# Attention block on one NeuronCore: queries and keys laid out token by token, and score and context matmuls spread between projection halves

## The chip, the core and the metric

The kernel runs on one core of one Trainium2 chip. The metric is the device time of one execution in microseconds (us). Three runs of the kernel before gave 2223.61, 2233.66 and 2239.39 us; the median is 2233.66 us. One further execution was taken by the hardware profiler; its own time was 2238.77 us and its span, from the first to the last instruction, 2236.9 us.

## What is computed

One pre-layernorm transformer block on 2048 tokens of width 1024, in float32. The attention is unusual: it is taken within each token, between its 32 heads, not between tokens. Each token thus has a 32 x 32 score matrix of its own.

```python
def attention(x):                                   # x: (1, 2048, 1024), already normalised
    q = (x @ wq.T + bq).reshape(B, S, 32, 32)       # heads h, head width d
    k = (x @ wk.T + bk).reshape(B, S, 32, 32)
    v = (x @ wv.T + bv).reshape(B, S, 32, 32)
    scores = einsum('bshd,bstd->bsht', q, k) / sqrt(32)
    return einsum('bsht,bstd->bshd', softmax(scores), v).reshape(B, S, 1024)

x = x + attention(layernorm(x))
h = layernorm(x)
x = x + (silu(h @ dq(w1).T) * (h @ dq(w2).T)) @ dq(w3).T   # hidden width 2752
```

Here dq rounds a weight to the 16 values of the NF4 code, per block of 64 elements with the block's largest magnitude as scale. The kernel does this rounding itself, on the chip.

## The kernel before

The program has two stages. The **attention stage** takes the first 617 us of the profiled execution, the **FFN stage** the rest. A third kind of work, the rounding of the FFN weights (the "background"), runs beside both.

**Tiles.** Tokens come in 16 tiles of 128. For tile i, `load_x` brings x into one of three `xt` buffers. `prepare(i)` normalises it into `xn` with three passes on ACT (ScalarE) and small steps on POOL (GpSimd). `split(i)` transposes `xn` on PE (TensorE) in eight blocks through two PSUM banks; ACT copies the result rounded to the shorter float32r format into `xh` (line 620) and DVE (VectorE) writes what the rounding lost into `xl` (line 621).

**Projections.** `Q(i, n)`, `K(i, n)` and `V(i, n)` each make one half (512 columns) of the queries, keys or values: 16 matmuls (line 648), for eight chunks of the input width and for both parts xh and xl, into one PSUM bank. Four banks go round for these halves, for the transposes of `split` and `keep`, and for the transposes of background weights (`ptw`). After the 16 matmuls the half is taken out: DVE transposes it in 32 x 32 blocks from PSUM to SBUF (line 665 for queries and keys, line 678 for values) and, after the second half, adds the bias. Queries and keys lie in `qd` and `kd` as 128 partitions x 32 x 32: in a group of 32 partitions the partition is the head width, the first free index is the head and the second the token. Values in `vd` lie with the token first, and each token has a 33rd column of ones, so that the context matmul also makes the softmax's sum.

**Scores and contexts.** `S(i, part)` issues 64 matmuls of 32 x 32 (line 696), one per token and group of 32 partitions; part 0 and part 1 are the halves of a tile. It reads `q[r, :, s]` and `k[r, :, s]`, that is, 32 elements 128 bytes apart in each partition. After part 1, DVE takes the maxima (line 733), subtracts them (line 735), ACT takes the exponential (line 741) and DVE transposes the result into `prT` (line 743). `G(i, part)` issues 64 matmuls (line 700) that weigh the values; after part 1, DVE divides by the sums (lines 758, 760), transposes into `cx` (line 768), adds the residual (line 771); SP, the queue of the loads and stores, writes x1 out and loads the next x tile; ACT and POOL normalise `cx`. Scores and contexts of all tiles use one PSUM tile `at` of four banks, one after the other. In the trace each of the 64 float32 matmuls has two records, so that a part appears as x128.

**Keep.** `keep(i)` transposes the normalised `cx` on PE (line 511), copies it out on ACT (line 512) and, for every second tile, forms four differences on DVE (line 527); all go to DRAM as operands of the FFN, which multiplies 2 x 2 blocks with seven products in place of eight.

**Background.** `advance(n)` issues n x 10/17 steps of the weight rounding: a pass of ACT (line 299) and one of DVE (lines 303, 305) for each of eight bands of code values, block maxima (line 271), reciprocals and scalings (lines 255, 259). A call of `advance` follows each projection half and each part of scores or contexts. `flush(1)` issues one piece of the finishing of a rounded weight: four transposes on PE (line 219) with a copy on ACT (line 220), or the differences on DVE (lines 226 to 235) and the store.

**What sets the order.** On PE the instructions run in the order in which the program writes them. On the other engines a planner places them, from the program's dependences; each engine then works through its own list in order. The order written for a tile i from 3 to 14 is

`prepare(i+1)  Q(i,0)  Q(i,1)  keep(i-2)  K(i,0)  G(i-1,0)  K(i,1)  G(i-1,1)  V(i,0)  S(i,0)  V(i,1)  split(i+1)  S(i,1)`

with `flush(1)` before `keep`, before `G(i-1,1)` and before `split`. After the loop, the first products of the FFN (`plain_block`, each `next` one group of four matmuls of line 391) alternate with `keep(14)`, `G(15, .)` and `keep(15)`. There, after `G(15,1)`, `held["behind"]` makes background steps start only behind the last normalisation. The first full FFN unit follows; its first sum is copied by ACT to `g` (line 1416).

A second, slower path of the same function serves inputs that the short format can't hold; it isn't run with these inputs. The profile numbers lines as in the listing.

## Time and profile before

| stretch, us from the start of the span | length | PE busy | DVE busy | ACT busy | granted PE clock |
|---|---|---|---|---|---|
| attention stage, 0 to 617 | 617.0 | 573.7 | 450.9 | 352.6 | 0.96 |
| of it twelve tiles, 145.48 to 566.50 | 421.0 | 398.9 | 327.5 | 238.4 | 0.97 |
| of it the end, 566.50 to 600 | 33.5 | 30.0 | 10.9 | 7.0 | 0.90 |
| into the FFN, 600 to 640 | 40.0 | 31.8 | 25.1 | 30.2 | 0.87 |
| FFN stage, 617 to 2237 | 1620.0 | 1593.4 | 927.2 | 934.6 | 0.99 |
| profiled execution, span | 2236.9 | 2167.1 | 1378.0 | 1287.2 | 0.98 |
| profiled execution, its own time | 2238.8 | | | | |

Busy time is the time in which an engine has at least one instruction under way. The granted clock is the mean share of full speed at which TensorE was allowed to run; in the trace it is either 1 or one half. A tile of the twelve is counted from its first score matmul to that of the next tile. In lines of groups, the name before the arrow is what is written, the names behind it what is read; then come sizes and count, busy time and mean nanoseconds of one, and the idle time of the engine just before with what ended it.

### The profile page before, as it was taken

The page shows a single profiled execution, that of the slowest core. Times are in us where ns is not written, and L with a number is a line of the kernel's source. Part 1 is how long each engine was busy: PE and PEld are TensorE (multiplying, and loading weights), DVE is VectorE, ACT ScalarE, POOL GpSimd, SP SyncE. Part 2 cuts the span into 40 slices and gives each one's busy share as a digit, 9 for nine tenths or more (in the row PEclk, how much of TensorE's full clock was granted, in tenths as well). Part 3 has the DMA queues.
Part 4 walks back from the last instruction along what each step waited for, and adds up shares of the span by engine and source line. Part 5 has one row for each costly group of instructions (what it writes and reads, how often), then busy time and mean ns, then how long its engine had stood idle before and what let it go on. Part 6 is the DMA issues. An engine that isn't in the chain of part 4 may idle for free.

```text
span 2236.9 us, 35174 instructions
## 1 busy us (share of the span) xinstructions
PE 2167.1 (97%) x14193; PEld 1173.4 (52%) x14193; DVE 1378.0 (62%) x1600; ACT 1287.2 (58%) x2529; POOL 302.2 (14%) x425
## 2 busy tenths in 40 slices
PE   7999999989989999999999999999999999999998
PEld 6777787778534444444444444444444444444432
DVE  6778777786377565576565665756666656653022
ACT  7566665662285756758657666676586575511200
POOL 2010010100001203104012021040130210401300
PEclk9899999999999999999999999999999999999999
DMA  8132323234558837579349596394883776974972
GB/s 292 40 101 93 117 65 115 95 98 144 216 193 294 172 141 180 163 280 252 137 141 210 206 283 149 124 214 162 308 207 133 181 190 224 269 236 136 255 290 96
DMA packets 154683, 402.72 MB, mean 180 GB/s; under 512 B 13648, under 2 KB 67920, under 8 KB 137360
## 3 DMA queue, kind: packets, MB, share of 16 engines
q1 hardware_dynamic: 113808, 326.92, 40.7%
q0 software_dynamic: 40704, 73.47, 19.7%
q8 instruction: 113, 1.85, 0.3%
q14 instruction: 58, 0.48, 0.1%
HBM read 227.07 MB, written 173.28 MB: 179 GB/s over the span
## 4 chain that ended last, share of the span: by engine, by line
PE 48%; issue 14%; DMA 5%; DVE 2%; ACT 2%; POOL 1%; DVEq 0%; POOLq 0%; ACTq 0%; SPq 0%
PE z L391 18%; PE q L391 8%; PE z L1511 8%; PE rr L391 4%; PE y L1511 4%; DMA wd<-wop 3%; DMA x1d<-acc 3%; PE r L1511 2%; PE po L1594 1%; PE ptw L219 1%; DVE r L305 1%; PE po L1605 1%; ACT wn L259 1%; POOL x1d L1526 1%; ACT acc L1524 0%
## 5 line engine op out<-in xcount | busy, mean ns | idle before, releaser
L299 ACT ACTIVATE sg<-wn 128x1024 int8<-128x1024 f32 (+1 forms) x520 | 542.5, 1052 | 138.6 <-DVE r L305 128.0
L305 DVE CUSTOM_DVE_ANT_0 r<-r,sg 128x1024 f32<-128x1024 f32 (+1 forms) x455 | 551.4, 1212 | 31.1 <-ACT sg L299 12.0
L1526 POOL DMA_DIRECT2D x1d<-acc x280 | 244.8, 900 | 1253.2 <-ACT acc L1524 1220.0
L391 PE MATMUL z<-xB,w 128*128 128x512 f32 x720 | 320.9, 595 | 3.5 <-ACT u L1430 2.1
L391 PE MATMUL z<-xT,w 128*128 128x512 f32 x656 | 297.5, 596 | 8.3 <-ACT g L1416 8.2
L391 PE MATMUL q<-xT,w 128*128 128x512 f32 x656 | 291.1, 592 | 0.0
L1511 PE MATMUL z<-w,h 128*128 128x512 f32 x496 | 230.5, 593 | 1.7 <-ACT acc L1524 1.5
L391 PEld LDWEIGHTS z<-xB,w 128*128 128x128 f32 x720 | 135.0, 191 | 163.5 <-issue 157.1
L259 ACT ACTIVATE wn<-wn,rc 128x64 f32<-128x64 f32 x736 | 189.0, 340 | 40.2 <-DVE rc L279 40.1
L391 PEld LDWEIGHTS z<-xT,w 128*128 128x128 f32 x656 | 124.1, 192 | 159.7 <-issue 149.0
L391 PEld LDWEIGHTS q<-xT,w 128*128 128x128 f32 x656 | 123.1, 190 | 148.4 <-issue 146.3
L303 DVE TENSOR_SCALAR r<-sg 128x1024 f32<-128x1024 int8 (+1 forms) x65 | 44.5, 684 | 194.7 <-PE ptw L219 194.4
L1511 PEld LDWEIGHTS z<-w,h 128*128 128x128 f32 x496 | 92.6, 190 | 112.7 <-issue 102.8
L1511 PE MATMUL y<-w,h 128*128 128x512 f32 x320 | 148.8, 592 | 0.0
L391 PE MATMUL rr<-xB,w 128*128 128x512 f32 x328 | 147.5, 592 | 0.0
L220 ACT COPY wop<-ptw 128x512 f32<-128x512 f32 (+1 forms) x130 | 76.2, 586 | 113.2 <-PE ptw L219 87.7
L1524 ACT COPY acc<-z 128x512 f32<-128x512 f32 x160 | 92.6, 581 | 70.7 <-PE z L1511 54.5
L1426 DVE TENSOR_TENSOR g<-g,rr 128x512 f32<-128x512 f32 x41 | 27.9, 681 | 168.4 <-PE rr L391 168.3
L259 ACT ACTIVATE r<-r,am 128x64 f32<-128x64 f32 x440 | 113.0, 343 | 8.9 <-DVE r L305 8.6
L271 DVE TENSOR_REDUCE am<-wn 128x16 f32<-128x1024 f32 (+1 forms) x65 | 78.6, 1209 | 48.0 <-ACT r L259 45.6
L648 PE MATMUL pj<-wv,xh 128*128 128x512 f32 x240 | 105.1, 438 | 1.2 <-issue 1.2
L648 PE MATMUL pj<-wv,xl 128*128 128x512 f32 x240 | 101.0, 421 | 0.0
(144 smaller groups left out, 2730.3 us busy)
## 6 DMA issues: line engine op xcount, KB each, us to landing
x1d<-acc POOLq DMA_DIRECT2D x280, 256.0 KB, 6.8
wd<-wop SPq DMA_DIRECT2D x31, 2048.0 KB, 8.5
w<-wd SPq DMA_DIRECT2D x41, 1280.0 KB, 7.0
wn<-in_w_dram SPq DMA_DIRECT2D x63, 512.0 KB, 6.0
xT<-xdT SPq DMA_DIRECT2D x28, 1024.0 KB, 7.6
xB<-xdB SPq DMA_DIRECT2D x24, 1024.0 KB, 6.7
w<-wd SPq DMA_DIRECT2D x44, 512.0 KB, 4.3
w<-wd SPq DMA_DIRECT2D x10, 1536.0 KB, 8.3
```

What stands on the lines that cost most here:

```text
L220: nc.scalar.copy(o[:q, first + half], pt[:q])
L259: nc.scalar.mul(dst[:, ts(n, BLOCK)], src[:, ts(n, BLOCK)], by[:, n : n + 1])
L271: nc.vector.tensor_reduce(am[:, :nb], v.rearrange("p (b e) -> p b e", e=BLOCK), AX.X, ALU.max, apply_absolute_value=True,)
L299: nc.scalar.activation(t, v, AF.Copy, bias=bias, scale=scale)
L303: nc.vector.tensor_scalar(r, t, top, low, ALU.min, ALU.max)
L305: nc.vector._custom_dve(TENSOR_ADD_SAT, out=r, in0=r, in1=t, s0=top, s1=low)
L391: nc.tensor.matmul(dst, w[:, k, :], xop[:, k, :], start=start and k == 0, stop=stop and k == 3, skip_group_check=True,)
L648: nc.tensor.matmul(ps, part[:, k, :], W[m][k // 2][:, k % 2, ts(n, TB)], start=k == 0 and part is xs[i][0], stop=k == KC - 1 and part is x ...
L1426: nc.vector.tensor_tensor(self.g0, self.g0, r, ALU.add)
L1511: nc.tensor.matmul(dst, side[n][:, ts(q, P)], w3T[g[2 * m]][:, W3[n]], start=start and m == 0, stop=stop and m == 1, skip_group_check=True,)
L1524: nc.scalar.copy(t, src)
L1526: nc.gpsimd.dma_start(x1d[8 * tbp + 2 * q + j][n], t, accum_op=ALU.add)
```

## The change

Four edits, all in the attention stage.

1. Queries and keys lie token first: the DVE transposes write through a view with the two free indices exchanged, the bias is broadcast along the other index, and the score matmuls read `q[r, s, :]` and `k[r, s, :]`.
2. `project` and `Q` get an argument `first`: something that is issued behind the 16 matmuls of a half and ahead of its transpose on DVE.
3. The order of the loop. For a tile i from 3 to 14 it becomes `Q(i,0)  S(i-1,1)  Q(i,1)  keep(i-2)  split(i+1)  K(i,0)  G(i-1,0)  K(i,1)  G(i-1,1)  prepare(i+2)  V(i,0)  V(i,1)  S(i,0)`, where S(i-1,1) is issued ahead of the transpose of Q(i,0). There is a `flush(1)` behind K(i,0) and behind each value half. The contexts of tile 1 move ahead of the loop.
4. The end: the second scores of the last tile and its contexts stand between the first products of the FFN; `held["behind"]` isn't set any more, and the calls of `advance` and `flush` there are placed anew.

```diff
-        def project(m, i, n, take):
+        def project(m, i, n, take, first=lambda: None):
...
+            first()
             take(n, ps)
             advance(1)
...
             t = work.tile([P, 32, NH], FP, tag=tag, name=f"{m}d")
+            by_head = t.rearrange("p s h -> p h s")
 
             def take(n, ps):
                 hs = ts(n, NH // 2)
-                nc.vector.transpose(t[:, hs], ps.rearrange("p (h d) -> p h d", d=D))
+                nc.vector.transpose(by_head[:, hs], ps.rearrange("p (h d) -> p h d", d=D))
                 if n:
                     nc.vector.tensor_tensor(
-                        t, t, bias.unsqueeze(2).to_broadcast([P, 32, 32]), ALU.add
+                        t, t, bias.unsqueeze(1).to_broadcast([P, 32, 32]), ALU.add
                     )
...
-                nc.tensor.matmul(at[r, b, ts(n, 32)], q[r, :, s], k[r, :, s], start=True, stop=True)
+                nc.tensor.matmul(at[r, b, ts(n, 32)], q[r, s, :], k[r, s, :], start=True, stop=True)
...
         prepare(3)
         V(1, 0)
+        V(1, 1)
         S(1, 0)
-        V(1, 1)
+        K(2, 1)
         S(1, 1)
-        K(2, 1)
         keep(0)
         split(3)
+        G(1, 0)
+        flush(1)
+        G(1, 1)
         for i in range(2, NT):
             last = i == NT - 1
             if i > 2:
+                Q(i, 0, lambda: S(i - 1, 1))
+                Q(i, 1)
+                keep(i - 2)
                 if not last:
-                    prepare(i + 1)
-                Q(i, 0)
-                Q(i, 1)
+                    split(i + 1)
+                K(i, 0)
                 flush(1)
-                keep(i - 2)
-                K(i, 0)
-            if last:
-                for name in ("B11", "B21"):
-                    load_op(name, 0)
-            G(i - 1, 0)
-            if i > 2:
+                G(i - 1, 0)
                 K(i, 1)
+                if last:
+                    for name in ("B11", "B21"):
+                        load_op(name, 0)
+                G(i - 1, 1)
+            if i + 2 < NT:
+                prepare(i + 2)
+            V(i, 0)
             flush(1)
-            G(i - 1, 1)
             if last:
...
-            V(i, 0)
-            S(i, 0)
             V(i, 1)
             flush(1)
-            if not last and i > 2:
-                split(i + 1)
-            S(i, 1)
+            S(i, 0)
             advance(2)
...
         plain = plain_block(w0, 0)
-        next(plain)
-        advance(1)
-        next(plain)
+
+        def piece(n):
+            got = next(plain)
+            advance(n)
+            return got
+
+        piece(1)
+        S(NT - 1, 1)
+        piece(2)
         keep(NT - 2)
-        advance(1)
-        next(plain)
+        piece(2)
+        piece(2)
         G(NT - 1, 0)
-        next(plain)
+        piece(2)
+        flush(1)
         G(NT - 1, 1)
-        held["behind"] = hook["normed"]
-        for _ in range(3):
-            next(plain)
-            advance(2)
+        piece(1)
+        flush(1)
+        piece(1)
+        hs = {0: piece(1)}
         keep(NT - 1)
-        hs = {0: next(plain)}
-        advance(2)
```

More of the change, by code (lines that the diff above doesn't have):

```diff
@@ L704, in forward, with Q @@
         qd, kd, prT, ats = {}, {}, {}, {}
-        def Q(i, n):
+        def Q(i, n, first=lambda: None):
             if not n:
                 qd[i] = qk("q", i, qb_sb)
-            project("q", i, n, qd[i][1])
+            project("q", i, n, qd[i][1], first)
         def K(i, n):
```

## The prediction

> **What bounds the kernel now.** First the busy shares: TensorE (PE) is busy nearly all the time, so a stretch gets shorter only if its matmuls do or its gaps close.

> ```profile
> PE 2167.1 (97%) x14193; PEld 1173.4 (52%) x14193; DVE 1378.0 (62%) x1600; ACT 1287.2 (58%) x2529; POOL 302.2 (14%) x425
> ```

> The change lies in the attention stage, the first 617 us. I cut it at the first scores of successive tiles and read engine times per stretch (span, busy of PE, PEld, DVE, ACT, POOL, granted clock, DMA).

> ```profile
> 217.49:253.15 35.66, 33.66 (x633) 27.40 (x633) 30.23 (x35) 22.25 (x44) 2.36 (x8) 0.95 0.35 120
> ...
> 287.41:319.89 32.48, 31.78 (x624) 25.79 (x624) 26.44 (x28) 21.42 (x50) 5.16 (x8) 1.00 0.21 66
> ...
> 145.48:566.50 421.02, 398.92 (x7556) 325.33 (x7556) 327.46 (x366) 238.44 (x487) 36.81 (x92) 0.97 0.33 108
> ```

> The last row holds twelve tiles: 421.02/12 = 35.08 us each, 22 us of gaps in all, DVE 327.46/12 = 27.3 us busy per tile. The first two rows show a dear and a cheap tile; DVE is idle 5.43 us in the one and 6.04 us in the other. The waits of PE in these twelve tiles (total, times, longest):

> ```profile
> PE sc L696 <- DVE pw L760: 10.7, 7, 3.0
> PE sc L696 <- issue: 4.6, 4, 1.9
> PE pj L648 <- ACT xh L620: 3.3, 6, 0.8
> PE sc L696 <- DVE rc L278: 2.2, 1, 2.2
> PE pj L648 <- DVE xl L621: 1.5, 6, 0.3
> ```

> Scores and contexts share the one `at` tile, so scores of a tile wait until the weighted contexts of the tile before (pw) are out of it. Last, the two kinds of small matmuls, as groups and in order of time:

> ```profile
> L696 PE MATMUL sc<-kd,qd 32*32 32x32 f32 x4096 | 67.6, 225 | 21.3 <-DVE pw L760 10.7 <-issue 8.4 <-DVE rc L278 2.2
> L700 PE MATMUL cx<-vd,prT 32*32 32x33 f32 x4096 | 43.9, 196 | 0.7 <-issue 0.7
> ```

> ```profile
> 314.75 1.29 PE L700 MATMUL cx<-vd,prT 32*32 32x33 f32 x128
> 315.96 0.50 PE L648 MATMUL pj<-wv,xh 128*128 128x512 f32 x1
> ...
> 319.89 2.03 PE L696 MATMUL sc<-kd,qd 32*32 32x32 f32 x128
> 321.85 0.50 PE L648 MATMUL pj<-wv,xh 128*128 128x512 f32 x1
> ```

> From its start to the start of what follows, a burst of contexts takes 1.21 us and a burst of scores 1.96, for the same 128 records, the same four diagonal 32x32 positions and the same walk over tokens; contexts even move one column more. The difference in the code is that contexts read 32 neighbouring elements per partition, scores read elements 128 bytes apart.

> **Part 1, the scores read neighbours.** 32 bursts x (1.96 - 1.21) = 24.0 us less PE, 18.0 of it in the twelve tiles, 6.0 outside. Bounds: nothing, if the stride isn't the reason, to 24.0. I take 24.0, since the context row is the same operation.

> **Part 2, the transposes write 128 bytes apart.** The stride moves to the output of DVE's 64 transposes of queries and keys.

> ```profile
> L678 DVE STREAM_TRANSPOSE vd<-pj 128x512 f32<-128x512 f32 x32 | 36.0, 1131 | 33.7 <-PE pj L648 33.7
> L768 DVE STREAM_TRANSPOSE cx<-pw 128x1024 f32<-128x1024 f32 x16 | 35.7, 2232 | 0.2
> ...
> L665 DVE STREAM_TRANSPOSE kd<-pj 128x512 f32<-128x512 f32 x32 | 22.5, 709 | 22.3 <-PE pj L648 22.3
> ...
> L743 DVE STREAM_TRANSPOSE prT<-pr 128x1024 f32<-128x1024 f32 x16 | 19.9, 1245 | 18.4 <-ACT pr L741 18.4
> ```

> Both transposes that write strided (they also read strided) take about 1.13 us per 512 elements, the others 0.71 or less. So one becomes 0.71 (nothing added) to 1.13 us; I take 1.13, the row with the same kind of write: +0.42 x 64 = 27 us of DVE, 1.7 per tile, 29.0 per tile in all. The bias add keeps its size and runs along contiguous elements (1.22 us either way, as the value bias at 1.22 shows).
> [...]

> **Part 3, the order on PE.** Per tile it becomes Q0, S1 of the tile before, Q1, eight transposes of `keep`, eight of `split` for the next tile, K0, G0, K1, G1, V0, V1, S0. No instruction is added. What PE alone needs: six halves at 3.8 (16 matmuls 0.233 apart, a little more after a burst) = 22.8; four bursts at 1.21 = 4.84; `keep` 0.79; `split` 0.97; weight transposes 17 x 0.44 / 12 = 0.62. Sum 30.0 us per tile, against 35.08.
> The wait on pw goes: two value halves lie before S0 instead of one (7.7 us; pw was at most 3.0 late with one). The waits on xh and xl go: they are now made a whole tile ahead. The DVE wait on POOL's norm is untouched. `prepare` moves behind the load of its own x tile: its first ACT pass queues behind the norm of cx, which itself follows a 2 to 4 us write, and the load lands in 3.9 us, so I cost it at nothing; were that cover gone, up to 4 us of ACT per tile stand ahead of copies that PE needs 10 us later, still nothing. On SP, the same copies are issued; the first FFN weights still stand ahead of the last x1d writes.
> What is late next: the second half of `split` needs the bank that Q1's transpose on DVE frees. In a full stretch, DVE has between pw and the score maximum: 2.2 (cx), 1.25 (residual), 2 x 1.13 (values), 1.15 (bias), 0.6 + 4 x 1.15 (weight steps), 3 x 0.6 (weight differences) = 13.9 us, and it starts them some 2 us after G1; PE needs 3 x 3.8 + 2 x 1.21 + 0.9 = 14.7 us for V0, V1, S0, Q0, S1. So the maximum comes about 1.2 us late, and then follow maximum 1.15, Q0 1.13, subtraction 1.15, Q1 1.13 = 4.6, where PE reaches that bank after 3.8 + 0.8 + 0.5 = 5.1. PE waits 0.7 us, more where weight steps pile up, nothing in tiles with few. Bounds for the wait per tile: 0, to 34.4 - 30.0 = 4.4, if DVE with 29.0 us of work can't get below its smallest idle of 5.43. I take 1.7 with its aftermath in the clock: 31.7 us per tile, nearer to the lower end, since most of DVE's idle time in these tiles (22.7, 19.5 and 11.6 us before the three kinds of projection transposes) is waiting for PE and shrinks with it.
> The aftermath: after PE's 1.13 us wait at 353.3 the granted clock of that tile was 0.95, and the value half behind it took 5.17 instead of 3.84. Seven such halves or groups cost 9.8 us in the twelve tiles. [...]
> Twelve tiles: 12 x (35.08 - 31.7) = 40.6 us.

> **Part 4, the ends.** The last tile's scores and contexts now lie between the pieces of the first FFN unit, and the weight steps no longer wait for the last norm.

> ```profile
> PE z L391 <- ACT g L1416: 8.2, 1, 8.2
> ```

> This is the wait at 621.7 us: ACT stood at weight scaling ahead of g's copy, behind DVE weight steps held until after the last norm. The first matmuls after it ran at the low clock (5.9 us for 3.43). In the new order ACT has only the two copies of `keep` ahead of g. I take 9 of these 10.7 us (0 to 10.7). At the start, G0 of tile 1 follows its scores after 1.8 us of transposes instead of 5.6; maximum, subtraction, exponential and transpose are 4.7 us, partly under the present 2.98 us wait for xn: +2 us (0 to 3). The rest of the FFN (PE 98% busy) stays.

> **Sum.** -40.6 - 6.0 - 9 + 2 = -53.6 us. The profiled execution took 2238.77 us (span 2236.9): 2185 us. The median shown, 2233.66, is 5 us lower; I leave the point there and let the range cover it. A difference under 1% (22 us) is about what can't be told from no change.

> **Rivals.**
> *PE's floor is reached* (DVE keeps up, or its transposes stay at 0.71): 12 x 5.08 = 61, + 6 + 10.7: 2161 us. For it: most idle time of DVE is waiting for PE. Against: 29.0 of 30.0 us.
> *DVE becomes the bound*: 34.4 us per tile; 12 x 0.7 = 8, + 6 + 9 - 2: 2218 us. For it: no tile had DVE idle under 5.4 us, and DVE takes its work in order.
> *The stride isn't the price of scores*: 24 us are lost from the forecast: 2209 us. Only the 33rd column and the tile read differ otherwise.
> *Slower: Q1's transpose stops PE at `split` in each tile and the clock falls with it.* It decides from a wait of 3.8 us per tile (30.0 + 3.8 + 1.3 > 35.1). With the 4.4 of above plus the share by which twelve low windows lengthen DVE's chain, say 5.4 us, and two low windows (2.6): 38.0 per tile, +35, less 13: 2261 us. Against: it needs more DVE work than the sum has.

> **How the numbers follow.** Forecast 0.48; floor 0.2; DVE bound 0.16; no gain from the stride 0.08; slower 0.08 (a part of which stays within 1%). Faster by over 1% means under 2211: forecast, floor, half of the stride case, a quarter of the DVE case and some luck in it: 0.78. Within 1%: 0.15. Slower: 0.07. The range goes from the floor (2161, less the 5 us of the median) to a little over the DVE case.

> **What would show it.** Score bursts near 1.2 us, projection transposes near 1.13, no wait of scores on pw, no wait of g, a new wait at pt (L618) or contexts on DVE, DVE over 85% busy in the tiles, tiles of 31 to 32.5 us. I am wrong if score bursts stay at 1.96, if the transposes cost much more than 1.13, or if waits on instructions grow as bursts get shorter.

## The result: 0.7% slower, and the profile after

The changed kernel takes 2248.84 us (median of 9 runs, 2240.77 to 2261.20) beside 2235.98 us of the kernel before (9 runs, 2223.61 to 2239.39): a ratio of 1.0067 with a 95% interval of 1.0050 to 1.0085. The forecast was 2185 us, its range ended at 2222. The loss is under the 1% that the prediction called hard to tell from no change; the interval tells it. The profiled execution took 2248.77 us, its span is 2247.0, 10.1 us more than before.

The page's busy times of the changed kernel; each engine with its busy time, its share of the span and its instructions:

```profile
PE 2154.5 (96%) x14193; PEld 1152.8 (51%) x14193; DVE 1396.2 (62%) x1599; ACT 1287.1 (57%) x2545; POOL 325.7 (14%) x425
```

TensorE works 12.6 us less than before and the kernel is longer, so its gaps grew by some 23 us. The groups of PE and of DVE in the changed kernel (busy time, mean ns of one, idle time before them with what ended it) show that the operations cost what the prediction took for them:

```profile
L702 PE MATMUL cx<-vd,prT 32*32 32x33 f32 x4096 | 43.0, 195 | 6.1 <-issue 3.0 <-DVE prT L745 3.0
L698 PE MATMUL sc<-kd,qd 32*32 32x32 f32 x4096 | 41.8, 193 | 1.9 <-issue 1.9
```

```profile
L667 DVE STREAM_TRANSPOSE kd<-pj 128x512 f32<-128x512 f32 x32 | 34.5, 1086 | 47.7 <-PE pj L648 46.7 <-PE pj L631 0.8
L667 DVE STREAM_TRANSPOSE qd<-pj 128x512 f32<-128x512 f32 x32 | 33.8, 1064 | 1.8 <-PE pj L648 1.8
```

Scores now cost the same as contexts (41.8 us against 67.6 before; from start to start a burst takes 1.21 to 1.22), and a projection transpose 1.06 to 1.09 us (0.71 before, 1.13 expected).

The twelve tiles are where the forecast's gain should have been. Three stretches of the changed kernel, each from a tile's first scores to the next tile's (stretch and its length, busy of PE, PEld, DVE, ACT, POOL, granted clock, DMA share, GB/s): a cheap tile, a dear one, and all twelve together.

```profile
234.33:264.69 30.36, 30.36 (x630) 24.60 (x629) 25.03 (x28) 15.69 (x21) 2.65 (x7) 1.00 0.40 139
511.28:551.91 40.63, 33.84 (x633) 26.80 (x632) 31.12 (x34) 26.30 (x57) 8.19 (x9) 0.87 0.18 62
158.53:586.73 428.20, 388.14 (x7553) 309.64 (x7553) 346.75 (x369) 248.65 (x511) 56.67 (x92) 0.94 0.33 109
```

The average is 428.20 / 12 = 35.68 us (35.08 before, 31.7 forecast), but no tile is average: four of the twelve take 30.4 to 32.6 us, seven 34.2 to 40.6, and one (38.5) waits for the norm. In the cheap tile PE is busy from end to end, at 30.4 us near the predicted floor of 30.0. DVE is busy 346.75 / 12 = 28.9 us per tile, the 29.0 that the prediction worked out. In the kernel before the tiles lay between 32.5 and 36.5. The waits of PE in the twelve tiles of the changed kernel (total, times, longest):

```profile
PE pt L618 <- DVE qd L667: 21.0, 14, 3.1
PE pj L648 <- ACT xT L512: 10.2, 7, 2.9
PE pt L618 <- ACT xn L585: 4.6, 2, 4.0
PE pj L648 <- DVE qd L667: 2.2, 1, 2.2
```

The waits on `pw`, `xh` and `xl` are gone, as predicted. In their place `split` (L618) waits for the banks that DVE's transposes of the two query halves free, and the first key half (L648) for a bank that ACT's copy of `keep` (L512) frees. What makes DVE late is read from its own list. DVE in the dear tile, in order of time (start, length, operation), from `pw` to the two query transposes:

```profile
505.56 1.22 DVE L762 TENSOR_TENSOR pw<-cx,rs 128x1024 f32<-128x1024 f32 x1
...
512.48 2.46 DVE L305 CUSTOM_DVE_ANT_0 r<-r,sg 128x1024 f32<-128x1024 f32 x2
...
515.86 1.22 DVE L305 CUSTOM_DVE_ANT_0 r<-r,sg 128x1024 f32<-128x1024 f32 x1
...
518.12 5.20 DVE L305 CUSTOM_DVE_ANT_0 r<-r,sg 128x1024 f32<-128x1024 f32 x4
523.24 1.22 DVE L735 TENSOR_REDUCE mx<-sc 128x32 f32<-128x1024 f32 x1
524.37 1.05 DVE L667 STREAM_TRANSPOSE qd<-pj 128x512 f32<-128x512 f32 x1
525.29 1.18 DVE L737 TENSOR_TENSOR pr<-sc,mx 128x1024 f32<-128x1024 f32 x1
526.41 1.01 DVE L667 STREAM_TRANSPOSE qd<-pj 128x512 f32<-128x512 f32 x1
```

Seven weight steps of line 305, and one of line 303 at 511.30 (in a part that is left out), stand between `pw` and the maximum. The last score matmul ends at 517.7; the maximum starts 5.5 us later, and what stands behind it in the list is late with it. PE in the same stretch (idle time before an instruction, and what ended it, in brackets):

```profile
525.57 1.09 PE L618 MATMUL pt<-ident,xn 128*128 128x128 f32 x4 [3.05 <-DVE qd L667]
527.48 1.12 PE L618 MATMUL pt<-ident,xn 128*128 128x128 f32 x4 [0.82 <-DVE qd L667]
531.51 0.80 PE L648 MATMUL pj<-wk,xh 128*128 128x512 f32 x1 [2.92 <-ACT xT L512]
```

The first four transposes of `split` start 0.15 us after DVE's transpose of the first query half ends (524.37 + 1.05), the other four behind that of the second. So it is in all seven tiles that wait here: 13.0 of the 21.0 us of the first row of waits stand ahead of the first four. The key half then waits for ACT, which is late too. Its list in the same stretch, the scalings of a weight, the exponential and the copies of `keep`:

```profile
527.09 2.96 ACT L259 ACTIVATE r<-r,am 128x64 f32<-128x64 f32 x12
529.95 1.04 ACT L743 ACTIVATE pr<-pr 128x1024 f32<-128x1024 f32 x1
530.90 1.04 ACT L512 COPY xT<-pt 128x512 f32<-128x512 f32 x2
```

That is 6.8 us of waiting of PE, and the key half behind it takes from 531.51 to 536.93, 5.4 us for 3.8, at a granted clock of 0.68. The same part of DVE's list in the kernel before, in the last of its twelve tiles:

```profile
530.57 1.21 DVE L760 TENSOR_TENSOR pw<-cx,rs 128x1024 f32<-128x1024 f32 x1
...
536.80 3.75 DVE L305 CUSTOM_DVE_ANT_0 r<-r,sg 128x1024 f32<-128x1024 f32 x3
...
544.58 1.22 DVE L733 TENSOR_REDUCE mx<-sc 128x32 f32<-128x1024 f32 x1
```

Three steps; before, no tile has more than three between the two, and the maximum starts 0.6 to 2.8 us behind the end of the scores. The changed kernel's tiles (steps between `pw` and the maximum, block maxima of line 271 included; from the end of the scores to the start of the maximum; first scores to first scores):

| tile | 3 | 4 | 5 | 6 | 7 | 8 | 9 | 10 | 11 | 12 | 13 | 14 |
|---|---|---|---|---|---|---|---|---|---|---|---|---|
| steps | 7 | 8 | 0 | 2 | 8 | 5 | 1 | 8 | 5 | 0 | 8 | 7 |
| maximum late by, us | 5.1 | 4.3 | 0.0 | 0.0 | 4.7 | 2.7 | 0.0 | 4.2 | 3.6 | 0.0 | 5.5 | 4.7 |
| length, us | 38.0 | 37.8 | 30.4 | 38.5 | 39.3 | 32.0 | 32.6 | 38.7 | 34.2 | 31.5 | 40.6 | 34.8 |

The number of steps hardly changed (passes of lines 303 and 305 in the twelve tiles: 69 before, 72 after); their place did: 14 of them stood between `pw` and the maximum before, 58 do now.

### The profile page after: what moved, and what is told of

Its sections match the earlier page's. It is cut to its first block, busy times and chain, and to the rows that moved or that the text cites. A ratio compares the mean times of both kernels' runs of the same rounds, so it can differ in the third digit from the quotient of the medians.

```text
span 2247.0 us, 35205 instructions
## 1 busy us (share of the span) xinstructions
PE 2154.5 (96%) x14193; PEld 1152.8 (51%) x14193; DVE 1396.2 (62%) x1599; ACT 1287.1 (57%) x2545; POOL 325.7 (14%) x425
## 3 DMA queue, kind: packets, MB, share of 16 engines
q0 software_dynamic: 40704, 73.47, 19.5%
## 4 chain that ended last, share of the span: by engine, by line
PE 47%; issue 25%; DVE 10%; DMA 7%; ACT 6%; POOL 4%; SPq 0%; DVEq 0%; POOLq 0%; ACTq 0%
PE z L391 15%; PE z L1519 7%; PE q L391 6%; PE pj L648 5%; PE y L1519 3%; DMA x1d<-acc 3%; PE rr L391 3%; POOL x1d L1534 2%; PE r L1519 2%; DVE r L305 2%; DVE cx L770 1%; PE po L1602 1%; PE ptw L219 1%; ACT sg L299 1%; PE pj L631 1%
## 5 line engine op out<-in xcount | busy, mean ns | idle before, releaser
L391 PE MATMUL z<-xB,w 128*128 128x512 f32 x720 | 321.1, 596 | 5.0 <-DMA w<-wd 3.5
L391 PE MATMUL z<-xT,w 128*128 128x512 f32 x656 | 297.9, 597 | 3.4 <-ACT u L1431 3.4
L391 PE MATMUL q<-xT,w 128*128 128x512 f32 x656 | 291.3, 592 | 0.0
L391 PEld LDWEIGHTS z<-xB,w 128*128 128x128 f32 x720 | 134.9, 191 | 165.7 <-issue 156.7
L391 PEld LDWEIGHTS z<-xT,w 128*128 128x128 f32 x656 | 124.1, 192 | 152.1 <-issue 147.8
L391 PEld LDWEIGHTS q<-xT,w 128*128 128x128 f32 x656 | 123.3, 190 | 149.5 <-issue 147.4
L391 PE MATMUL rr<-xB,w 128*128 128x512 f32 x328 | 147.5, 592 | 0.0
L648 PE MATMUL pj<-wk,xh 128*128 128x512 f32 x224 | 102.3, 457 | 14.7 <-ACT xT L512 12.6
L271 DVE TENSOR_REDUCE am<-wn 128x16 f32<-128x1024 f32 (+1 forms) x65 | 78.4, 1207 | 44.5 <-ACT r L259 41.8
L391 PEld LDWEIGHTS rr<-xB,w 128*128 128x128 f32 x328 | 61.5, 190 | 73.7 <-issue 73.7
```

The lines of the kernel that those rows point to most:

```text
L271: nc.vector.tensor_reduce(am[:, :nb], v.rearrange("p (b e) -> p b e", e=BLOCK), AX.X, ALU.max, apply_absolute_value=True,)
L391: nc.tensor.matmul(dst, w[:, k, :], xop[:, k, :], start=start and k == 0, stop=stop and k == 3, skip_group_check=True,)
L648: nc.tensor.matmul(ps, part[:, k, :], W[m][k // 2][:, k % 2, ts(n, TB)], start=k == 0 and part is xs[i][0], stop=k == KC - 1 and part is x ...
```

## The experiments

Ratios are to the kernel before, run on the same chip, with 95% intervals. "Tile" is the mean from S(3,0) to S(15,0) in the trace; "FFN begins" is the start of the first `q` product (L391), "FFN" the time from there to the end. Tile and FFN come from one profiled execution each. How far such figures are apart by chance: DVE's list is the same in the kernel before and in `e7_new_end` up to 549 us, ACT's up to 500, yet their S(3,0) starts at 145.48 and 141.98 us, and the nine tiles behind it are 0.29 us shorter on average in the second. `e4`, `e15` and `e16` ran once each and are read by their tiles alone.

| kernel | ratio | tile | FFN begins | FFN |
|---|---|---|---|---|
| before | 1 | 35.09 | 618.1 | 1618.8 |
| after | 1.0067 [1.0050, 1.0085] | 35.68 | 626.3 | 1620.7 |
| e1_layout | 1.0040 [1.0022, 1.0058] | 35.26 | 623.8 | 1619.8 |
| e2_order | 1.0006 [0.9992, 1.0020] | 35.06 | 617.8 | 1614.8 |
| e9_scores_only | 0.9994 [0.9985, 1.0004] | 34.54 | 614.4 | 1617.2 |
| e10_transposes_plain | 1.0009 [0.9993, 1.0025] | 34.88 | 619.6 | 1624.3 |
| e3_split_late | 1.0089 [1.0057, 1.0121] | 36.20 | 629.4 | 1621.5 |
| e5_k_first | 1.0036 [1.0021, 1.0052] | 35.23 | 621.2 | 1618.4 |
| e13_fill | 1.0031 [1.0014, 1.0048] | 35.54 | 627.2 | 1618.9 |
| e8_steps_075 | 1.0163 [1.0146, 1.0180] | 33.78 | 605.3 | 1669.5 |
| e14_steps_085 | 1.0122 [1.0085, 1.0160] | 34.58 | 620.8 | 1639.7 |
| e6_old_end | 1.0050 [1.0032, 1.0069] | 35.25 | 631.8 | 1613.0 |
| e7_new_end | 1.0017 [1.0001, 1.0033] | 34.68 | 614.1 | 1624.9 |
| e18_order_k_first_old_end | 1.0013 [1.0001, 1.0024] | 34.97 | 621.8 | 1615.0 |

### Which part makes it slower: layout and order apart

`e1_layout` is the kernel before with the token-first layout alone, `e2_order` the changed kernel with the old layout.

```diff
-                nc.vector.transpose(by_head[:, hs], ps.rearrange("p (h d) -> p h d", d=D))
+                nc.vector.transpose(t[:, hs], ps.rearrange("p (h d) -> p h d", d=D))
...
-                nc.tensor.matmul(at[r, b, ts(n, 32)], q[r, s, :], k[r, s, :], start=True, stop=True)
+                nc.tensor.matmul(at[r, b, ts(n, 32)], q[r, :, s], k[r, :, s], start=True, stop=True)
```

> Only the token-first layout of queries and keys (strided transposes, scores that read neighbours), in the order of before. Theory A (the changed kernel loses its gain where the transposes of split stand right behind the second query half, in the bank that DVE has not yet freed): the layout is good by itself; score bursts 1.2 us instead of 1.96, tiles about 34 us instead of 35.1, 10 to 20 us less than before. Theory B (the strided transposes fill DVE, whatever the order): tiles 35.5 to 36.5 us, 5 to 15 us more than before.

> Only the new order, with the old layout (transposes 0.71 us, scores 1.96 us). Theory A: the wait of split on the second query transpose stays, a little shorter (DVE saves 0.4 us per transpose); tiles 36 to 37 us, 5 to 20 us more than the changed kernel. Theory B: the wait goes with the strided writes, under 0.5 us per tile; tiles about 32.5 us, 25 to 35 us less than the changed kernel.

The layout alone loses 0.40%, although PE's busy time falls from 2167.1 to 2150.6 us, and the order alone gives nothing (1.0006). For `e1_layout` the total came as its theory B had it, the tile a little shorter; neither theory of `e2_order` held. So the layout, the part that was to bring 24 us of PE time, carries most of the loss, and the order brings none of the gain that closed waits should. `e2_order` has the same clumps of steps as the changed kernel (7, 8, 0, 2, 8, 5, 1, 8, 5, 0, 8, 7), and its tiles are as long as those of the kernel before, which has no clumps: the new order with its clumps is no dearer than the old one without them.

### The two halves of the layout

`e9_scores_only` is the kernel before with scores that read neighbours; `e10_transposes_plain` is the changed kernel with transposes that write as before. In both the scores are of other elements than they should be, with the same operations and sizes; the cut is that of `e10_transposes_plain`.

```diff
-                nc.vector.transpose(by_head[:, hs], ps.rearrange("p (h d) -> p h d", d=D))
+                nc.vector.transpose(t[:, hs], ps.rearrange("p (h d) -> p h d", d=D))
```

> The kernel before, scores reading neighbours, while the transposes write as before and the scores are thus of other elements: the price of the stride on PE alone, without the dearer transposes. If PE bounds the tiles: score bursts 1.2 us, 20 to 26 us less than before. Theory C: the bursts get shorter and the waits behind them longer; 0 to 12 us less than before.

> The changed kernel, transposes of queries and keys writing neighbours (0.71 us) as before, scores reading neighbours too and thus of other elements: the new order and the short bursts without the dearer transposes. Theory C: DVE has 1.7 us per tile less; tiles 33.5 to 34.5 us, 15 to 25 us less than the changed kernel. Theory A: waits at split 0.8 us shorter per tile; 8 to 12 us less.

Per tile this gives the price of each half in both orders. Cheap scores take 1.5 us of PE time off a tile; the tile gets shorter by 0.55 us (35.09 to 34.54) in the old order and 0.18 (35.06 to 34.88, within chance) in the new one. Dear transposes add 4 x 0.36 = 1.4 us of DVE time; the tile gets longer by 0.72 (34.54 to 35.26) and 0.80 (34.88 to 35.68). In whole runs cheap scores are worth nothing that can be told (0.9994 in the old order; 1.0006 to 1.0009 in the new one), and dear transposes cost 0.46% (old order: e9 to e1) and 0.58% (new order: e10 to after): without them the changed kernel is level with the kernel before (1.0009). So `e9_scores_only` came out at the low end of its theory C, and `e10_transposes_plain` gained 13 us, between its two theories. The twelve tiles of `e9_scores_only`:

```profile
147.90:562.40 414.50, 380.79 (x7556) 306.61 (x7556) 324.74 (x366) 238.18 (x487) 39.56 (x92) 0.97 0.33 110
```

PE is busy 18.1 us less than before (398.92 to 380.79), the 18.0 that the prediction worked out; the stretch is only 6.5 us shorter. The gaps grew from 22.1 to 33.7 us. A microsecond of DVE was worth more here than one of PE, with PE busy 95% of the time and DVE 78%.

### Moving the place of the wait

`e3_split_late` puts `split` behind the second value half (and `prepare` behind it); `e5_k_first` puts the first key half ahead of `keep` and `split`.

```diff
                 Q(i, 1)
+                K(i, 0)
                 keep(i - 2)
                 if not last:
                     split(i + 1)
-                K(i, 0)
                 flush(1)
```

> The changed kernel with split(i+1) moved behind the second value half (prepare(i+2) behind it), nothing else. Theory A: no wait at split or at the first key half above 0.5 us per tile, granted clock near 1, tiles 31 to 32.5 us instead of 35.7, 35 to 50 us less than the changed kernel. Theory B: DVE stays behind and stops PE somewhere else (contexts, or the bank of another half); tiles 34 us or more.

> The changed kernel with the first key half ahead of keep and split (both then stand behind it), nothing else. Theory C (the tiles are bounded by what DVE and ACT do in their own order, weight steps among it; PE only waits at another place when the order on PE changes): the wait moves to contexts or another half, tiles stay at 34.5 to 36 us, within 10 us of the changed kernel. Theory A (the place of split behind the second query half is what costs): 3.8 us more slack end the wait, tiles 31 to 32.5 us, 35 to 50 us less than the changed kernel.

Neither removes the time. The longest waits of PE in the twelve tiles, of `e3_split_late` and then of `e5_k_first`:

```profile
PE pj L648 <- ACT xh L620: 29.0, 12, 6.2
```

```profile
PE pt L618 <- ACT xT L512: 30.6, 8, 5.5
```

As theory B said, in `e3_split_late` PE no longer waits for the query transposes at `split` but for `xh`, and the tile is 36.20 us. In `e5_k_first` it waits at `split` for ACT's copies of `keep`; the tile is 35.23, and the whole kernel regains about half of its loss (1.0036), far from the 35 to 50 us that theory A promised. The waiting instruction is where the lateness becomes visible, not where it arises.

### Is it the low clock?

`e13_fill` keeps PE occupied near the wait with 16 idle transposes between `keep` and `split`.

```diff
                 keep(i - 2)
+                for _ in range(16):
+                    nc.tensor.transpose(hook["at"][:, 0, 384:512], ident, ident)
                 if not last:
                     split(i + 1)
```

> The changed kernel with 16 idle transposes of the identity (1.6 us of PE at full clock, into columns of the score tile that nobody reads) between keep and split in tiles 3 to 15. If the half clock after the waits at split is a good part of the loss: the granted clock of the tiles rises from 0.93 to 0.97 or more, heavy tiles get shorter by 2 us or more, cheap ones longer by 1.6; in all 5 to 15 us less. If DVE's lateness alone sets the tiles, heavy tiles stay and the cheap ones get longer: 5 to 15 us more.

The mean granted clock of the whole run rises from 0.976 to 0.987, and in the twelve tiles from 0.94 to 0.97; the FFN begins at 627.2 us (626.3 without). The fill is not perfect: its first transpose waits for the subtraction, which reads the same tile, 18.6 us in eight tiles. The four cheap tiles get 0.9 us longer on average, the other eight 0.7 us shorter (by 3.2 in the dear one, but longer by 3.4 in the last), and the mean tile takes 35.54 us instead of 35.68 although 16 transposes were added to it. The ratio of whole runs is 0.36% better than that of the changed kernel, some 8 us, as the first expectation had it; its 2 us per heavy tile did not show. So the low clock is a part of what a wait costs (in the dear tile of the changed kernel the key half took 5.4 us for 3.8 at a clock of 0.68), though not what makes PE wait. The profiled execution's attention stage shows less than the whole runs (it is one of the slower executions, 2247.84 us against a median of 2243.92); how much belongs to the clock was not separated.

### Taking the weight steps out

`e4_no_weight_steps` leaves the background out of tiles 3 to 14 of the changed kernel and makes it up later; `e8_steps_075` and `e14_steps_085` issue three quarters and 0.85 of it there (with a factor in place of the return); `e14_steps_085` also raises `RATE`, which sets how many steps go with each stretch of the FFN, from 0.69 to 0.85.

```diff
+        if lent.get("off"):
+            return
         lent["turns"] += n * TURN
...
+            lent["off"] = 2 < i < NT - 1
```

> The changed kernel without background steps in tiles 3 to 14 (the weight rounding is then made in the FFN stage, which waits for it: only the tiles are to be read). Theory A, with weight steps as what makes DVE late: no wait at split above 0.5 us, tiles 30 to 31 us. If the four banks and the order of DVE alone were to blame, waits of 1 to 3 us stay and tiles are 33 us or more.

> The changed kernel with three quarters of the weight steps in tiles 3 to 14 (some 20 steps, 1.8 weights, are left to the FFN stage). Theory C: each step less takes 1.15 us of DVE and 1 us of ACT out of the tiles; tiles 32 to 33.5 us instead of 35.7; in all 15 to 35 us less than the changed kernel, unless the FFN stage must wait for its weights. Theory A: waits at split stay above 2 us per tile, tiles 34.5 us or more.

> The changed kernel with 0.85 of the weight steps in tiles 3 to 14, and 0.85 in place of 0.69 as the rate of steps in the FFN stage. Theory C: tiles about 34.5 us, attention 10 to 15 us shorter; with the higher rate the FFN stage catches up with one weight in its first 60 us and loses under 10 us: 0 to 15 us less than the changed kernel. If the weights are due right at the beginning of the FFN stage, it loses 20 us or more there and the total is longer.

Without steps PE bounds the tiles of the changed kernel: from S(4,0) at 194.44 to S(14,0) at 494.09 there are ten tiles of 29.97 us and no gap at all.

```profile
194.44:494.09 299.65, 299.65 (x6241) 241.61 (x6240) 207.25 (x210) 90.90 (x131) 29.35 (x80) 1.00 0.24 73
```

That this is the predicted floor of 30.0 is partly luck. The sum counted 0.62 us of weight transposes, and without steps no weight is finished, so there are none in these tiles; on the other hand the six halves take 23.2 us in place of 22.8, and the rest is a little longer too. "Without steps" thus means without any background work, on PE as well as on DVE and ACT.

With 0.75 of the steps a tile takes 33.78 us, with 0.85 34.58, with all of them 35.68. The steps have to be done somewhere, though: what the tiles gained was lost behind them, and more. Waits of PE in the FFN of `e8_steps_075`:

```profile
PE z L1520 <- DMA w<-wd: 25.8, 5, 5.7
PE z L391 <- DMA w<-wd: 8.4, 1, 8.4
```

Its products wait for weights that come too late, and the FFN is 49 us longer. The 0.85 run loses 19 us there and gains 5.5 ahead of it, not the 10 to 15 expected.

### The same for the kernel before

The last question is whether the steps already set the tiles of the kernel before. `e15_before_no_steps` is that kernel without steps in tiles 3 to 14 (the edit as above), `e16_layout_no_steps` adds the layout.

> The kernel before, without any weight step in tiles 3 to 14 (the steps left out there are made up later, so that the FFN starts late and the time of the whole run says little; the tiles are read). Theory: the weight steps in the lists of DVE and ACT set the tiles of the kernel before too. Then its tiles fall from 35.1 us to what PE alone needs with scores of 1.96 us, which is 30.0 + 2 x 0.75 = 31.5 us; 31.3 to 32 expected. Rival: before, the order on PE (pw ahead of the scores, xh and xl ahead of Q0) sets them; then at most the 22 us of gaps of the twelve tiles change little and they stay above 33.5 us.

> The same with the token-first layout alone added. Theory: without the weight steps the price of each operation on PE shows in full, so the tiles fall by 2 x 0.75 = 1.5 us against the run beside it, to 30.0 to 30.5 us, though the transposes on DVE are dearer. Rival: the dearer transposes stand on the path that sets the tile even without the weight steps; then less than 0.7 us of the 1.5 shows.

Ten tiles of each, from S(4,0) to S(14,0):

```profile
179.00:495.32 316.32, 315.88 (x6241) 258.56 (x6241) 197.52 (x211) 90.50 (x130) 23.45 (x80) 1.00 0.23 69
```

```profile
183.12:492.46 309.34, 301.32 (x6242) 242.05 (x6241) 212.81 (x211) 90.11 (x130) 23.47 (x80) 1.00 0.23 71
```

Without steps the kernel before needs 31.63 us per tile, and PE is busy all but 0.04 of it, within the 31.3 to 32 expected of PE alone. So its waits on `pw`, `xh` and `xl`, too, come from the steps; its order is nearly no obstacle without them. With the layout 30.93: PE's busy time falls by the full 1.46 us per tile, but only 0.70 of it shows, at the edge of what the rival allowed, since 0.6 us per tile returns as waits on `xl` (4.3 us in ten tiles) and `xh` (1.9). That the dearer transposes stand ahead of `xl` in DVE's list is the likely reason; it was not tested. The new order on top brings 29.97: without background work the prediction's plan works.

### The ends, and do the losses add?

`e6_old_end` is the changed kernel with the end of before, `e7_new_end` the kernel before with the end of the changed one. `e18_order_k_first_old_end` combines the order with what had helped one by one: old layout, key half first, old end.

```diff
+            if last:
+                S(i, 1)
             advance(2)
...
-        piece(1)
-        S(NT - 1, 1)
-        piece(2)
+        next(plain)
+        advance(1)
+        next(plain)
         keep(NT - 2)
...
+        held["behind"] = hook["normed"]
```

> The changed kernel with the end of before (second scores of the last tile ahead of the FFN products, steps held behind the last norm). Theory E (the new end is worth the 20 us that it shows, and the 10 us lost in the FFN stage come from weight steps being at another point when it begins): the wait on g of 8 us is back, the FFN stage shorter by 5 to 12 us than the changed kernel's; in all 5 to 15 us more than the changed kernel. If the FFN's loss belongs to something else in the attention stage, it stays and the total is 15 to 20 us more.

> The kernel before with only the end of the changed kernel. Theory E: no wait on g, attention 8 to 15 us shorter, a part of it given back in the FFN stage; 3 to 15 us less than before. If the gain of the end is only shifted (the same weight steps are merely waited for later): within 3 us of before.

> The changed order of the tiles with the first key half ahead of keep and split, with the old layout and the end of the kernel before. If the parts add up as measured one by one (order 1.0006, key half first -0.31%, end of before -0.17%), the ratio to the kernel before is 0.996, and this is the fastest of the versions (some 2227 us). Rival: the parts share one cause, the weight steps that have to be done by the end of the attention stage, and don't add; then it is 0.999 to 1.002.

The new end loses 0.17% on the kernel before, with an FFN 6.1 us longer, and with the old end the changed kernel's FFN is 7.7 us shorter: what the end gains, the FFN gives back. Behind the product that waits on `g`, the FFN takes 1605 to 1608 us in the five kernels with the old end (before, e1, e6, e9, e18) and 1611 to 1621 in the seven with the new one and all steps. In whole runs the two ends can't be told apart on the changed kernel (1.0050 and 1.0067), where both expectations of `e6_old_end` had a loss; the wait on `g` comes back there with 3.3 us of its 8.2. Added up, the parts of `e18` should have given 0.996; it measured 1.0013, so they don't add, as its rival said. The reason that the rival gives, that the steps have to be finished and that whatever frees one place for them fills another, fits e8, e14 and these runs, but nothing tested it by itself. No version is clearly faster than the kernel before.

## Why the prediction was wrong

The forecast's sum beside the traces, by stretch. V(3,1) (3.8 us) and `split(4)` (0.97) now lie ahead of S(3,0) and not behind it; these 4.8 us are taken out of the first row and out of the third.

| stretch | predicted | measured |
|---|---|---|
| start to S(3,0) | -4.5 (six bursts) + 2 | 158.53 - 145.48 - 4.8 = +8.2 |
| twelve tiles | -40.6 | 428.20 - 421.02 = +7.2 |
| S(15,0) to the product behind the wait on `g` | -1.5 - 9 | 43.01 - 63.45 + 4.8 = -15.6 |
| rest of the FFN | 0 | 1617.26 - 1606.95 = +10.3 |
| sum | -53.6 | +10.1 |

**The prices of Parts 1 and 2 were right.** Scores 1.21 to 1.22 us per burst, transposes 1.06 to 1.09. Here the stride cost 0.36 us of 1.07 in a transpose that writes 128 bytes apart, and 0.75 us of 1.96 per burst in the scores that had read so; no run shows why. Right as a price, Part 2 was wrong as a weight: the prediction booked 27 us of DVE's busy time and let them cost almost nothing, but in whole runs the dear transposes cost 0.46 to 0.58%, 10 to 13 us. That is the loss against the kernel before; what follows is why the gain stayed out.

**The step that failed is in Part 3, "What is late next".** It summed DVE's work between `pw` and the maximum with "0.6 + 4 x 1.15 (weight steps)", five steps, found the maximum "about 1.2 us late" and took a wait of 1.7 us with its aftermath. The mean number of steps was right: 59 in twelve tiles, 4.9 per tile. The distribution was not: 0 to 2 steps in four tiles, 5 to 8 in eight. Eight steps are three more than assumed, 9.2 us of DVE time in place of 5.2; the tiles with few gain nothing from their spare time, because PE can't run under its floor. So the maximum was late by 2.9 us on average (0.0 in four tiles, 2.7 to 5.5 in the others), and the two waits at `split` together are the lateness less 1.1 to 1.7 us in the seven tiles that have them. A tile cost 5.71 us above what it takes without background, not 1.7; of these 68.5 us in all, 55.6 lie in the eight tiles with 5 to 8 steps. The prediction said "more where weight steps pile up" and gave it no number. It also let only the second half of `split` wait, for the second query transpose; the longer wait stands ahead of the first half, for the first one. The same happened in ACT's list: in the dear tile twelve scalings stand ahead of the exponential and of the copies of `keep`, the wait of the key half that the prediction hadn't named.

Shown is that the background work sets the tiles (e4, e15) and that within the changed kernel the late tiles are those with many steps. That the clumping is what costs is argued from this: no run spread the same steps evenly, and `e2_order`, with the same clumps, is as long per tile as the kernel before. DVE's share and ACT's were not separated either, as each step has a pass on both.

**"PE's floor" was the wrong reference for the saving.** The prediction compared 30.0 us with the 35.08 of before, as if all the difference were there to be had. With e15 and e4 the account of a tile is: before, 31.63 for PE and 3.45 for the steps; after, 29.97 for PE and 5.71 for the steps. PE got 1.66 us shorter and the steps 2.26 dearer: 12 x 0.60 = 7.2 us, the second row of the table. Of the 5.71 us, 3.34 are gaps of PE and 2.37 are PE's own time above its 29.97: by estimate some 0.6 for the weight transposes, the rest work at half clock (the mean granted clock of these tiles is 0.94). Of the 3.45 before, 1.80 are gaps and 1.65 PE's own time. At most 1.66 x 12 = 20 us were at stake unless the steps became cheaper too, which is what 31.7 assumed (1.7 for 3.45) and no run shows.

**The start was mis-sized.** The loss was taken as +2 (0 to 3); without the 4.5 us that six bursts saved it is 12.7. The gaps of PE before S(3,0) grew from 17.7 to 26.3 us: contexts on `prT` 3.0 (the wait that had been expected), the key half on `keep` 2.4, `split` on the query transposes 1.9, and 3.7 instead of 0.9 us of waits on issue. The rest, some 4 us, is PE's own time, with a clock of 0.93 before and 0.89 after. e4 begins its tiles as late (157.6) and e2 nearly (155.3), so it is the order, not the steps of tiles 3 to 14; some 3.5 us can be chance, as e7 shows. Which of the moves costs how much was not separated.

**The end gained more than predicted, and the FFN did not stay.** The wait on `g` went (from the `q` product to the next, 11.84 us became 3.43). Waits of PE in the FFN after that point, changed kernel:

```profile
PE z L1519 <- ACT acc L1532: 4.6, 6, 1.2
PE z L391 <- DMA w<-wd: 3.5, 1, 3.5
PE z L391 <- ACT u L1431: 3.4, 1, 3.4
```

Before they were 2.9, none and 2.1 us. All waits there are 17.9 us against 10.5; with the low clock behind the 3.4 and 3.5 us ones (0.66 from 766 to 776 us, 0.76 from 2003 to 2010), this makes up most of the 10.3 us. The runs with either end show that it goes with the end; through which engine's list was not shown.

**The rivals.** The slower one (0.08) named the mechanism, DVE's query transpose stopping PE at `split` with a falling clock. The stop came in seven tiles (in an eighth, which has no `split`, at the key half) and not "in each"; in six of the seven the clock fell there (at 173.18, 210.73, 316.54, 422.35, 459.90 and 524.75 us), in the seventh, tile 8, it stayed at 1.00; the twelve tiles lost 3.3 us of waits each (39.3 us in all), and the sum was +10 us, not +22. Its counter-argument, that "it needs more DVE work than the sum has", was the error: DVE had no more work than the sum said, only unevenly spread. "DVE becomes the bound" took 34.4 us per tile from the smallest idle time of DVE; that smallest time was no bound. DVE is idle for only 0.77 us in tile 8 of the changed kernel, which takes 32.0 us, and for 9.51 us in the dear one. It was busy 81% of the twelve tiles, not over the 85% that the prediction looked for.

## What to carry to other kernels

Where an in-order engine also does background work, count tile by tile, in the changed program's own list, what stands between the event that releases and the operation that is waited for: a wait begins only where lateness exceeds the slack, so the mean of a clumped list can understate it. Before pricing a saving on the busiest engine, run the kernel without the background: here that split a tile into 31.6 us of PE and 3.5 of steps, and showed that work moved from a 95% busy PE to a 78% busy DVE can lose. When a wait is moved twice and the time stays, leave its place and look for what makes its producer late.

## What the runs showed of the hardware that was not expected

With idle work on PE (`e13_fill`) the mean clock of the profiled execution was 0.987 instead of 0.976, and whole runs got 0.36% shorter.

The waits of scores on "issue" differ from kernel to kernel, and not by the length of the bursts alone: with the long bursts 8.4 us in the kernel before, 3.1 in `e7_new_end` and 1.0 in `e2_order`; with the short ones 12.2 in e1, 13.4 in e9, 11.8 in `e6_old_end` and 1.9 in the changed kernel. What they are was not tried.
